# Projecting the first two units' attention values one unit at a time in 64 x 128 tiles of TensorE instead of two units at once in 64 x 32 tiles

## The chip, the cores and the metric

The kernel runs on one core of a Trainium2 chip. The metric is the device time of one execution in microseconds (us); several executions are timed and their median is given, and one more is recorded by the hardware profiler. All data are 32-bit floats.

## What is computed

The reference is one transformer block on two batches of 1024 tokens of 256 features: self-attention, cross-attention to a context of 154 tokens, and a gated feed-forward layer, each behind a layer norm and with a residual sum. Only the self-attention matters here:

```python
def _attention(xq, xkv, wq, wk, wv, wo, bo):
    q = (xq @ wq).reshape(B, S, N_HEADS, D_HEAD)
    k = (xkv @ wk).reshape(B, T, N_HEADS, D_HEAD)
    v = (xkv @ wv).reshape(B, T, N_HEADS, D_HEAD)
    attn = jnp.einsum('bihd,bjhd->bhij', q, k) * scale
    attn = jax.nn.softmax(attn, axis=-1)
    out = jnp.einsum('bhij,bjhd->bihd', attn, v).reshape(B, S, D_ATTN)
    return out @ wo + bo

h = _layernorm(x, ln1_g, ln1_b)
x = _attention(h, h, sa_wq, sa_wk, sa_wv, sa_wo, sa_bo) + x
```

There are 16 heads of 64 features, so `wq`, `wk` and `wv` are 256 x 1024.

## The kernel before, in words

The self-attention works in units. A unit is one batch and one pair of heads, so there are 16 units, and each needs 128 columns of queries, keys and values. The layer-normed and transposed activations of a batch lie in `hT`; its 128 partitions hold two halves of the tokens (partitions 0 to 63 and 64 to 127), each with its 256 features in four chunks of 64 (`NH` = 4). A projection therefore contracts over 64 rows at a time and uses the two halves of the array's rows for the two token halves.

Each unit is done in 8 steps `p` (two halves of 4), so unit 0 is steps 0 to 7, unit 1 steps 8 to 15. In one pass of the loop over `p` (L1294):

- `self_first(p)` (L676) multiplies queries with keys into two score tiles (`scores`, L491, on TensorE, "PE" in the profile), and VectorE (DVE) takes row maxima of each (L684). There are two score tiles in all, so the scores of a step wait until ScalarE (ACT) has done the exponents of the step before.
- The stores that the last step left behind are then issued (`flush(stores)`, L1301): copies from PSUM on ACT.
- `then()` issues the exponents (L509, ACT), the join of the step before on GpSimd (POOL) and ACT (`join`, L627), and the exchange of maxima and sums between partitions by four small DMAs on SyncE's (SP's) queue (L519).
- DVE turns the weighted exponents of earlier steps (`turn_group`, L647).
- `load_ahead` and the table `ahead` put weight loads on SP's queue: the keys' and queries' weights of unit 1 in steps 0 and 1 (L1286 and L1287).
- Last comes one larger piece of TensorE work: either half a unit's weighted sum of the values (`self_values`, L652, from step 7 on), or a piece from the list `work` (`run_work`, L573). Small side pieces, such as the context's keys (`context_keys`, L756) and a transposition of rows (L194), go along with the latter.

The order is written out by hand (`tc.manual_schedule`); each engine works through its own instructions in that order.

`work` begins with the second half of unit 0's queries (L1291) and two pieces of values (L1292); step 0 adds the queries and keys of unit 1 (`self_beside`, L697). So steps 0 to 4 each take one piece: queries of unit 0, values, values, queries of unit 1, keys of unit 1. Steps 5 and 6 find the list empty; step 6 adds the keys of two more pairs of heads for the cross-attention, one into a bank of the pool `sum_tile`, the other into one of `mm_tile`.

A piece of values (`project_self_values`, L394) takes a quarter of the tokens for two units at once: for each of two tiles of 128 tokens per half, four chunks, two halves and four groups of 32 tokens it multiplies 64 x 32 of `hT` (the stationary side) with 64 x 256 of `wv`. That is 64 matmuls in tiles of 64 rows by 32 columns of the array. Each matmul appears as two records in the trace. The result fills two PSUM banks (`two_banks`, L359); the pool `mm_tile` has only two, which queries, keys and values share, so a piece can begin only after the copies of the piece before. The store is four ACT copies of 256 columns to `held_v`, two for each unit. `held_v` has three places for units' values in turn (`unit_values`, L421) and a fourth that holds the current unit's values with the partition halves swapped (`move_values`, L424, in the sixth step of each unit). The weights `wv` are loaded for two units together, the next ones in step 7.

The prologue (L1260 to L1283) makes the first queries and keys with `project_both` (L362) in tiles of 64 rows by 128 columns, with 128 moving columns; line L369 in the profile.

Of the kernel before, what the change touches and what calls it, by code (L numbers as in the profile page):

```python
# [13 lines left out]
P = 128  # L14
# [4 lines left out]
def tile_transformer_block(ctx: ExitStack, tc: tile.TileContext, a: dict, out: bass.AP):  # L19
    nc = tc.nc  # L20
# [12 lines left out]
    GT = 4  # L33
    NG = NT // GT
    NC = D // P
    HR = P // 2
    NH = D // HR
# [32 lines left out]
    def mm_tile(name):  # L70
        return ps_m.tile([P, HB], F32, tag="mm", name=name)
# [25 lines left out]
    row_of, r = {}, 0  # L97
# [39 lines left out]
    wsl, wo = {}, {}  # L137
# [30 lines left out]
    for n in names[2:]:  # L168
        own = rows[row_of[n] - n_cols:row_of[n] - n_cols + n_of[n], :]
        p = HR if n in twice else P  # L170
# [45 lines left out]
    hT, vs, qk, oT = {}, {}, {}, {}  # L216
# [103 lines left out]
    def add_biases(kind, b):  # L320

        bo = {"sa": "sa_bo", "ca": "ca_bo", "ff": "ff_b2"}[kind]

        def add(t):
            xs = xt[b, t // GT][:, t % GT, :]
            nc.gpsimd.tensor_tensor(xs, xs, bias[bo], ALU.add)

        later.extend(lambda t=t: add(t) for t in range(NT))
        if b == B - 1 and kind != "ff":
            later.append(lambda: load_bias({"sa": "ca_bo", "ca": "ff_b2"}[kind]))  # L330

    def norm_beside(kind, b):

        after = {"sa": None, "ca": "sa", "ff": "ca"}[kind]
        stats, deviation, normalize, turn = norm_pieces(kind, b)
        n = 1 if narrow(kind, b) else 2
        lag = {}  # L340
        for fns, first in ((turn, 3), (stats, 0), (deviation, 1), (normalize, 2)):
            for i, fn in enumerate(fns):
                t = i if fns is stats else 2 * i + 1
                lag.setdefault(first + t // n, []).append((fn, fns is turn))
        for k in range(NT // n + 3):
            tiles = tile_order(kind)[k * n:(k + 1) * n]
            needs = [(after, b, half, t) for half in range(NQ) for t in tiles if after]

            def step(fns=lag[k]):
                slow.extend(fn for fn, _ in fns if fn in stats)  # L350
                done = [fn() for fn, _ in fns if fn not in stats]
                return next((fn for fn in done if fn), None)

            side.append((any(turns for _, turns in lag[k]), needs, step))
        if not narrow(kind, b):
            side.append((False, (), lambda: add_biases(kind, b)))


    def two_banks(name):  # L359
        return [mm_tile(f"{name}_{r}") for r in range(2)]  # L360

    def project_both(pq, wt, h, m, t0=0, n=S // 2, at=0):  # L362


        for c in range(NH):
            for f in range(0, P, m):
                for r in range(2):
                    own = slice(r * HR, (r + 1) * HR)
                    nc.tensor.matmul(  # L369
                        pq[r][f:f + m, at:at + n], lhsT=wt[own, c, f:f + m],  # L370
                        rhs=h[own, c, t0:t0 + n], start=(c == 0), stop=(c == NH - 1),
                        tile_position=(r * HR, f),
                    )

    def take_both(dst, pq, mul=None, t0=0, n=S // 2, shared=False):

        for r in range(2):
            k0, own = r * S // 2 + t0, pq[r][:, :n]
            if mul is not None:
                if shared and r:  # L380
                    nc.vector.tensor_scalar(
                        dst[:, k0:k0 + n], own, mul, 1.0, op0=ALU.mult, op1=ALU.mult)
                else:
                    nc.scalar.activation(dst[:, k0:k0 + n], own, AF.Copy, scale=mul)  # L384
                continue

            dk = dst.rearrange("p (h n j) -> p n h j", h=2, j=KB)[:, k0 // QG:(k0 + n) // QG]
            own = own.rearrange("p (n h j) -> p n h j", h=2, j=KB)
            if shared and r:
                nc.vector.tensor_copy(dk, own)  # L390
            else:
                nc.scalar.copy(dk, own)

    def project_self_values(b, pr, i):  # L394

        own = [unit_values(b, pr + j) for j in range(2)]
        pv = two_banks(f"pv_sa{b}_{pr}_{i}")
        wt, h = wsl["sa", pr, "v"], hT["sa", b]
        for e in range(2):
            for c in range(NH):  # L400
                for r in range(2):
                    half = slice(r * HR, (r + 1) * HR)
                    for f in range(0, P, KB):
                        t0 = (2 * i + e) * P + f
                        nc.tensor.matmul(  # L405
                            pv[r][f:f + KB, e * VC:(e + 1) * VC], lhsT=h[half, c, t0:t0 + KB],
                            rhs=wt[half, c, :], start=(c == 0), stop=(c == NH - 1),
                            tile_position=(r * HR, f),
                        )

        def store():
            for j in range(2):
                for r in range(2):
                    t0 = r * GT + 2 * i
                    nc.scalar.copy(
                        own[j][:, t0:t0 + 2, :],
                        pv[r].rearrange("p (e j d) -> p j e d", e=2, j=2)[:, j])

        return store

    def unit_values(b, pr):  # L421
        return held_v[:, (b * NPAIR + pr + 2) % 3]

# [7 lines left out]
    def costing(n, fn):  # L431

        fn.banks = n
        return fn

    def self_unit(b, pr):

        qk["sa", b, pr] = (
            p2.tile([P, S], F32, tag="QT", name=f"q_sa{b}_{pr}"),
            p2.tile([P, S], F32, tag="KT", name=f"k_sa{b}_{pr}"),  # L440
            (unit_values(b, pr), held_v[:, 3]),
        )

    def self_queries(b, pr, m=KB, t0=0):
        pq = two_banks(f"pq_sa{b}_{pr}")
        project_both(pq, wsl["sa", pr, "q"], hT["sa", b], m, t0, S // 2 - t0)
        return lambda: take_both(qk["sa", b, pr][0], pq, scale, t0, S // 2 - t0)

    def self_pieces(b, pr):


        def q():
            self_unit(b, pr)
            return self_queries(b, pr)

        def k():
            pk = two_banks(f"pk_sa{b}_{pr}")
            project_both(pk, wsl["sa", pr, "k"], hT["sa", b], KB)
            return lambda: take_both(qk["sa", b, pr][1], pk)

        return [costing(2, q), costing(2, k)]

    def value_piece(b, pr, i):
        return costing(2, lambda: project_self_values(b, pr, i))
# [20 lines left out]
    def out_order(kind):  # L485

        return [t for t in tile_order("ff" if kind == "ca" else "ca") if t % 2 == 0]
# [70 lines left out]
    work, outs = [], []  # L558
# [37 lines left out]
    def out_pieces(kind, b, half, tiles):  # L596
        outs.extend(lambda t=t: out_piece(kind, b, half, t) for t in tiles)

    units = [(b, pr) for b in range(B) for pr in range(NPAIR)]
# [97 lines left out]
    def self_beside(ui):  # L697

        nxt = self_pieces(*units[ui + 1]) if ui + 1 < NU else cross_pieces(*units[0])
        if ui + 1 < NU:  # L700
            if ui % 2 == 0 and ui:
                work.append(value_piece(*units[ui], 1))
            work.extend(nxt)
            if ui % 2:
                work.append(value_piece(*units[ui + 1], 0))
        else:

            work.extend(nxt[:1])
            held.extend(nxt[1:])
        if ui >= HP:  # L710
            ob, og = divmod((ui - HP) // HP, NQ)
            t0 = (ui % HP) * 2
            out_pieces("sa", ob, og, out_order("sa")[t0:t0 + 2])
        if ui == 1:
            norm_beside("sa", 1)
        if ui in (4, 6):
            add_biases("sa", (ui - 4) // 2)
        if ui == NPAIR + 1:
            norm_beside("ca", 0)
# [106 lines left out]
    def cross_pieces(b, pr):  # L826

        return [costing(2, lambda: cross_queries(b, pr, KB)), costing(1, lambda: context_values(b, pr))]
# [405 lines left out]
    with tc.manual_schedule():  # L1234
# [11 lines left out]
        own = [ps_s.tile([P, 2, HB], F32, tag="s", name=f"first_{r}") for r in range(2)]  # L1246
# [42 lines left out]
        side.extend((True, (), lambda pr=pr: context_keys(pr, sum_tile)) for pr in range(2))  # L1289
        side.append((True, (), turn_rows))  # L1290
        work.append(costing(2, lambda: self_queries(*units[0], P, 2 * P)))  # L1291
        work.extend(value_piece(*units[0], i) for i in range(2))  # L1292

        for p in range(SA):  # L1294
            if p % (2 * SH) == 0:
# [19 lines left out]
            h, hg = divmod(p, SH)  # L1315
            ui, n = divmod(p, 2 * SH)
# [6 lines left out]
            if hg == LAG:  # L1323
                f = (ui - NPAIR // 2 - 1) * EC
# [4 lines left out]
                if n == SH + LAG and ui in (0, 1, NU - 1):  # L1329

                    pr = {0: 2, 1: 4, NU - 1: 6}[ui]
# [3 lines left out]
        for c in range(CA):  # L1335
# [13 lines left out]
            ui, n = divmod(c, len(CG))  # L1349
# [83 lines left out]
        for k in range(2 * FU):  # L1433
            c = CA + k
# [17 lines left out]
            while n_left > 0 and sums:  # L1452
                fn, n = sums.pop(0)
# [51 lines left out]
```

## Time and profile before

| | |
|---|---|
| median of 3 runs | 1078.62 us (1077.93 to 1078.73) |
| profiled execution | 1076.39 us |
| its span, first to last instruction | 1074.6 us |
| PE busy / weight loads (PEld) busy | 1059.0 us (99%) / 711.8 us (66%) |
| DVE, ACT, POOL busy | 882.7, 645.5, 774.7 us |
| mean granted TensorE clock | 0.998 |
| values of the self-attention (L405) | 2048 records, 60.7 us |
| scores of the self-attention (L498) | 4096 records, 261.4 us |

The profile comes from one execution. "Busy" is the time in which an engine had an instruction in work. A row of a timeline or group names the source line, engine, output<-inputs, the tile of the array (rows*columns), the shape of the moving data and the number of records; brackets give how long the engine had stood before it, and what ended that. PEclk is the share of the full clock that TensorE was granted. The chain of waits is followed back from the last instruction of the execution. A DMA's landing is counted from its issue.

### The profile page before, as it was taken

How to read it: one execution, taken by the hardware profiler on the slowest of the kernel's cores; microseconds unless marked ns; L12 is line 12 of the kernel's file. 1: busy time of each engine (PE TensorE's matmuls, PEld its weight loads, DVE VectorE, ACT ScalarE, POOL GpSimd, SP SyncE). 2: the span in 40 equal slices, each digit the busy share in tenths (PEclk: the TensorE clock that was granted, in tenths of full speed). 3: DMA queues.
4: the chain of work that ended last, by engine and by line, in shares of the span. 5: the costliest groups of instructions: out<-in, count | busy, mean ns of one | idle time of the engine just before them, and what ended most of it. 6: DMA issues, size and time to landing. Idle time of an engine off the chain costs nothing.

```text
span 1074.6 us, 48887 instructions
## 1 busy us (share of the span) xinstructions
PE 1059.0 (99%) x20324; PEld 711.8 (66%) x20324; DVE 882.7 (82%) x1321; ACT 645.5 (60%) x2098; POOL 774.7 (72%) x1652
## 2 busy tenths in 40 slices
PE   8999999999999999999999999999999999999998
PEld 6366756656556655665775655566766667788998
DVE  5789999998989989999999899968877887655554
ACT  5666677677667666676776676665556564342331
POOL 2677777777777777677777777776666876499884
PEclk9999999999999999999999999999999999999999
DMA  3132121121121111111102101125776545000000
GB/s 101 31 79 54 25 67 48 24 73 26 30 50 42 34 47 33 44 33 34 44 14 53 44 14 38 33 54 137 173 180 166 124 107 114 16 5 16 20 10 30
DMA packets 86046, 60.97 MB, mean 57 GB/s; under 512 B 32122, under 2 KB 74562, under 8 KB 85826
## 3 DMA queue, kind: packets, MB, share of 16 engines
q1 hardware_dynamic: 84450, 57.07, 21.9%
q8 instruction: 160, 2.62, 1.0%
q10 hardware_dynamic: 1376, 0.79, 0.2%
q14 instruction: 60, 0.49, 0.2%
HBM read 27.91 MB, written 2.10 MB: 28 GB/s over the span
## 4 chain that ended last, share of the span: by engine, by line
PE 86%; DVE 3%; DMA 3%; POOL 3%; SPq 2%; issue 1%; ACT 1%; POOLq 0%; DVEq 0%; ACTq 0%
PE s L498 18%; PE po L550 18%; PE py_ca L472 5%; PE py_sa L472 5%; PE pv_sa L405 5%; PE pq_sa L369 5%; PE pk_sa L369 5%; PE poc L921 4%; PE pb L1042 4%; PE pq_ca L369 4%; PE pq L1187 3%; DMA st<-st 3%; PE sc L841 2%; PE pa L1042 2%; PE pc L1042 2%; SPq L519 2%
## 5 line engine op out<-in xcount | busy, mean ns | idle before, releaser
L622 POOL TENSOR_SCALAR p<-p,rd,ee 128x512 f32<-128x512 f32 x512 | 390.4, 768 | 97.7 <-DVE rd L612 97.3
L509 ACT ACTIVATE p<-s,st 128x512 f32<-128x512 f32 x512 | 345.0, 686 | 181.2 <-DVE st L684 177.6
L684 DVE TENSOR_REDUCE st<-s 128x2 f32<-128x1024 f32 x256 | 308.7, 1206 | 60.9 <-issue 22.7
L647 DVE STREAM_TRANSPOSE pT<-p 128x1024 f32<-128x1024 f32 x256 | 302.4, 1218 | 0.9 <-POOL p L622 0.9
L498 PE MATMUL s<-k_sa,q_sa 64*32 64x512 f32 x4096 | 261.4, 594 | 5.1 <-ACT p L509 4.4
L550 PE MATMUL po<-pT,held_v 64*32 64x256 f32 x8192 | 242.3, 376 | 0.9 <-DVE pT L647 0.5
L550 PEld LDWEIGHTS po<-pT,held_v 64*32 64x32 f32 x8192 | 178.8, 106 | 71.3 <-issue 22.6
L498 PEld LDWEIGHTS s<-k_sa,q_sa 64*32 64x32 f32 x4096 | 93.0, 107 | 94.8 <-issue 39.6
L858 ACT ACTIVATE p<-sc,neg 128x154 f32<-128x154 f32 x256 | 96.1, 404 | 79.2 <-DVE rden L866 75.2
L869 POOL TENSOR_SCALAR p<-p,rden 128x154 f32<-128x154 f32 x256 | 96.9, 399 | 51.7 <-DVE rden L866 51.4
L509 ACT ACTIVATION_READ_ACCUMULATOR p<-s,st 128x1 f32 x512 | 104.0, 203 | 0.0
L527 POOL TENSOR_TENSOR dd<-st 128x8 f32<-128x8 f32 x128 | 25.5, 200 | 66.8 <-DMA st<-st 63.0
L405 PE MATMUL pv_sa<-sa_wv,hT_ln 64*32 64x256 f32 x2048 | 60.7, 376 | 0.0
L472 PE MATMUL py_ca<-ca_wo,o_ca 128*128 128x256 f32 x256 | 60.2, 383 | 0.0
L472 PE MATMUL py_sa<-sa_wo,o_sa 128*128 128x256 f32 x256 | 59.7, 386 | 0.1
L847 DVE TENSOR_REDUCE neg<-sc 128x6 f32<-128x924 f32 (+1 forms) x48 | 47.8, 996 | 14.5 <-PE sc L841 14.5
L369 PE MATMUL pq_ca<-hT_ln,ca_wq 64*64 64x512 f32 (+1 forms) x544 | 59.1, 590 | 0.5 <-DVE st_ln L242 0.5
L472 PEld LDWEIGHTS py_sa<-sa_wo,o_sa 128*128 128x128 f32 x256 | 47.4, 190 | 18.1 <-issue 4.4
L369 PE MATMUL pk_sa<-hT_ln,sa_wk 64*32 64x512 f32 x960 | 57.5, 590 | 0.9 <-ACT q_sa L384 0.9
L369 PE MATMUL pq_sa<-hT_ln,sa_wq 64*32 64x512 f32 (+1 forms) x976 | 58.0, 586 | 0.0
L405 PEld LDWEIGHTS pv_sa<-sa_wv,hT_ln 64*32 64x32 f32 x2048 | 44.5, 106 | 18.1 <-issue 5.2
L858 ACT ACTIVATION_READ_ACCUMULATOR p<-sc,neg 128x1 f32 x256 | 56.5, 221 | 0.0
(155 smaller groups left out, 1471.9 us busy)
## 6 DMA issues: line engine op xcount, KB each, us to landing
wf<-pT_ca SPq DMA_DIRECT2D x128, 128.0 KB, 2.4
st<-st SPq DMA_DIRECT2D x512, 1.0 KB, 1.8
held_v<-held_v SPq DMA_DIRECT2D x32, 256.0 KB, 3.7
sa_wq<-in_L_xattn_sa_wq_dram SPq DMA_DIRECT2D x32, 128.0 KB, 3.6
sa_wk<-in_L_xattn_sa_wk_dram SPq DMA_DIRECT2D x32, 128.0 KB, 3.0
sa_wv<-in_L_xattn_sa_wv_dram SPq DMA_DIRECT2D x16, 256.0 KB, 4.5
ca_wq<-in_L_xattn_ca_wq_dram SPq DMA_DIRECT2D x32, 128.0 KB, 3.5
wf<-in_L_xattn_ff_w_dram SPq DMA_DIRECT2D x12, 256.0 KB
```

The costliest lines, as they stand in the source:

```text
L369: nc.tensor.matmul(pq[r][f:f + m, at:at + n], lhsT=wt[own, c, f:f + m], rhs=h[own, c, t0:t0 + n], start=(c == 0), stop=(c == NH - 1), tile ...
L405: nc.tensor.matmul(pv[r][f:f + KB, e * VC:(e + 1) * VC], lhsT=h[half, c, t0:t0 + KB], rhs=wt[half, c, :], start=(c == 0), stop=(c == NH - ...
L472: nc.tensor.matmul(py[:, e * D:(e + 1) * D], lhsT=o[:, i, (t + e) * P:(t + e + 1) * P], rhs=wo[kind][:, g * HP + i, :], start=(i == 0), st ...
L498: nc.tensor.matmul(sc[a4 * KB:(a4 + 1) * KB, j, :], lhsT=q[r, c:c + KB], rhs=k[r, h * HB:(h + 1) * HB], start=True, stop=True, tile_positi ...
L509: nc.scalar.activation(pr[:, j, :], sc[:, j, :], AF.Exp, bias=st[:, 0, 0, i, j:j + 1], accum_out=st[:, 0, 1, i, j:j + 1],)
L550: nc.tensor.matmul(po[a2][d:d + KB, :QH // 2], lhsT=v[e][r, t, d:d + KB], rhs=pT[r, d // DH * NK + n, :], start=(t == 0 and e == 0), stop= ...
L622: nc.gpsimd.tensor_scalar(pr[:, j, :], pr[:, j, :], own["rd"][:, c:c + 1], own["ee"][:, 0, c:c + 1], op0=ALU.mult, op1=ALU.mult,)
L647: nc.vector.transpose(halves[h][:, :, c:c + KB], slots[p]["p"][i].rearrange("p j (n k) -> p (j n) k", k=KB))
L684: nc.vector.tensor_reduce(st[:, 0, 0, i, :], sc[i], AX.X, ALU.max, negate=True)
L858: nc.scalar.activation(pr_[:, j, i, :T], sc[:, j, i * T:(i + 1) * T], AF.Exp, bias=neg[:, j, i:i + 1], accum_out=den[:, j, i:i + 1],)
L869: nc.gpsimd.tensor_scalar(pr_[:, j, i, :T], pr_[:, j, i, :T], rden[:, j, i:i + 1], 1.0, op0=ALU.mult, op1=ALU.mult,)
L1042: nc.tensor.matmul(into[:, :BT], lhsT=lhs, rhs=wh[pair][i], start=first, stop=True, skip_group_check=True)
```

## The change

The new function `project_unit_values` projects the values of one unit alone: the stationary side is 64 x 128 of `hT`, the moving side 64 x 128 of `wv`, in tiles of 64 rows by 128 columns of the array, `n` tiles of 128 tokens per half in one call. Its store copies `n` x 128 columns for each half. Unit 0 is done in two such pieces (two tiles of tokens each) in the places of the two old pieces. Unit 1 follows as one piece of four tiles of tokens behind the queries and keys of unit 1 in the list `work`. All later units are projected as before.

```diff
+    def project_unit_values(b, pr, i0, n):
+
+        own = unit_values(b, pr)
+        pv = two_banks(f"pv_sa{b}_{pr}_{i0}")
+        h, c0 = hT["sa", b], pr % 2 * P
+        wt = wsl["sa", pr - pr % 2, "v"][:, :, c0:c0 + P]
+        for i in range(i0, i0 + n):
+            for c in range(NH):
+                for r in range(2):
+                    half = slice(r * HR, (r + 1) * HR)
+                    nc.tensor.matmul(
+                        pv[r][:, i * P:(i + 1) * P], lhsT=h[half, c, i * P:(i + 1) * P],
+                        rhs=wt[half, c, :], start=(c == 0), stop=(c == NH - 1),
+                        tile_position=(r * HR, 0),
+                    )
+
+        def store():
+            for r in range(2):
+                t0 = r * GT + i0
+                nc.scalar.copy(
+                    own[:, t0:t0 + n, :],
+                    pv[r][:, i0 * P:(i0 + n) * P].rearrange("p (t d) -> p t d", d=P))
+
+        return store
+
@@ -459,6 +484,9 @@
+    def unit_value_piece(b, pr, i0, n):
+        return costing(2, lambda: project_unit_values(b, pr, i0, n))
 
     def value_piece(b, pr, i):
         return costing(2, lambda: project_self_values(b, pr, i))
@@ -701,6 +729,8 @@
             work.extend(nxt)
+            if ui == 0:
+                work.append(unit_value_piece(*units[1], 0, GT))
             if ui % 2:
                 work.append(value_piece(*units[ui + 1], 0))
@@ -1289,7 +1319,7 @@
         work.append(costing(2, lambda: self_queries(*units[0], P, 2 * P)))
-        work.extend(value_piece(*units[0], i) for i in range(2))
+        work.extend(unit_value_piece(*units[0], i, 2) for i in (0, 2))
```

## The prediction

> **What bounds the kernel now.** First the page: span, engines, chain.
>
> ```profile
> span 1074.6 us, 48887 instructions
> ...
> PE 1059.0 (99%) x20324; PEld 711.8 (66%) x20324; DVE 882.7 (82%) x1321; ACT 645.5 (60%) x2098; POOL 774.7 (72%) x1652
> ...
> PE 86%; DVE 3%; DMA 3%; POOL 3%; SPq 2%; issue 1%; ACT 1%; POOLq 0%; DVEq 0%; ACTq 0%
> ```
>
> TensorE (PE) is busy 99% and holds 86% of the chain that ended last. The changed work lies in the first 60 us, so I next read the timeline of PE there. Columns: start, length (us), engine, line, out<-in, tile, shape, count. One `matmul` of the code is two records.
>
> ```profile
> 9.47 1.16 PE L369 MATMUL first<-hT_ln,sa_wq 64*128 64x128 f32 x16
> 10.47 1.06 PE L369 MATMUL first<-hT_ln,sa_wk 64*128 64x128 f32 x16
> ...
> 17.51 1.95 PE L498 MATMUL s<-k_sa,q_sa 64*32 64x512 f32 x32 [0.65 <-DVE k_sa L390]
> 19.39 2.00 PE L369 MATMUL pq_sa<-hT_ln,sa_wq 64*128 64x256 f32 x16
> ...
> 21.99 1.96 PE L498 MATMUL s<-k_sa,q_sa 64*32 64x512 f32 x32
> 23.74 3.66 PE L405 MATMUL pv_sa<-sa_wv,hT_ln 64*32 64x256 f32 x128
> 27.33 1.34 PE L760 MATMUL pk<-ctxT,ca_wk 96*128 96x320 f32 x4
> 28.61 1.95 PE L498 MATMUL s<-k_sa,q_sa 64*32 64x512 f32 x32
> 30.35 3.66 PE L405 MATMUL pv_sa<-sa_wv,hT_ln 64*32 64x256 f32 x128
> 33.94 1.34 PE L760 MATMUL pk<-ctxT,ca_wk 96*128 96x320 f32 x4
> 35.21 1.95 PE L498 MATMUL s<-k_sa,q_sa 64*32 64x512 f32 x32
> 36.95 3.64 PE L369 MATMUL pq_sa<-hT_ln,sa_wq 64*32 64x512 f32 x64
> 40.52 0.24 PE L194 MATMUL p_rows<-ident,rows 28*128 28x28 f32 x1
> 40.69 1.97 PE L498 MATMUL s<-k_sa,q_sa 64*32 64x512 f32 x32
> 42.45 3.85 PE L369 MATMUL pk_sa<-hT_ln,sa_wk 64*32 64x512 f32 x64
> 45.89 2.13 PE L498 MATMUL s<-k_sa,q_sa 64*32 64x512 f32 x32
> 50.48 3.60 PE L498 MATMUL s<-k_sa,q_sa 64*32 64x512 f32 x32 [2.46 <-ACT p L509]
> 54.00 2.42 PE L760 MATMUL pk<-ctxT,ca_wk 96*128 96x320 f32 x8
> 56.35 1.95 PE L498 MATMUL s<-k_sa,q_sa 64*32 64x512 f32 x32
> ```
>
> Each row of scores (L498) opens a step p: p=0 at 17.51, p=1 at 21.99, then 28.61, 35.21, 40.69, 45.89, 50.48 (p=6), 56.35. In steps 1 to 4 PE has no gap: work of PE sets their length. Step 5 has scores alone, and PE stands 2.46 us until the exponents (ACT L509) free the score banks. The scores of step 6 then take 3.60 us where the others take 1.95. The windows of the trace show why (PEclk is the third column from the end):
>
> ```profile
> 47.05:50.46 3.41, 0.97 (x23) 0.06 (x7) 2.74 (x4) 1.89 (x6) 2.02 (x3) 1.00 0.04 4
> 50.46:53.88 3.42, 3.40 (x32) 0.62 (x32) 3.24 (x4) 1.42 (x6) 2.49 (x7) 0.50 0.02 3
> ```
>
> PE worked 0.97 of 3.41 us, and for the next 3.41 us the granted clock was 0.50. So the gap costs 2.46 us and 1.65 us more (3.60 - 1.95). The chain of waits passes there:
>
> ```profile
> 48.98 1.22 ACT p L509 x3
> ...
> 50.48 3.70 PE s L498 x32
> ...
> 54.20 1.24 DVE st L684
> ...
> 55.47 0.03 ACT p L509
> ```
>
> Later, from 102.3 us on, PE has hardly a gap, so I take time won before it as kept to the end:
>
> ```profile
> 102.30:700.00 597.70, 595.76 (x14592) 364.61 (x14596) 551.35 (x630) 411.49 (x1236) 448.75 (x933) 1.00 0.16 39
> ```
>
> **The change, part by part.**
>
> *Removed:* the two 64*32 pieces of steps 1 and 2, from start to next start 3.59 us each (27.33 - 23.74 and 33.94 - 30.35), 7.18 us.
>
> *Added:* unit 0 alone in steps 1 and 2 (16 matmuls, 32 records each), unit 1 in step 5 (64 records), as 64*128 tiles with 128 moving columns. The trace has this very form: 16 records take 1.00 us from 9.47 to 10.47, so 62.5 ns each. That is 2.0, 2.0 and 4.0 us, together 8.0: PE does 0.8 us more, but 4.0 of it where it stood.
>
> *Change of tile shape:* scores overlap the 64*32 values by 0.21 us (21.99 + 1.96 - 23.74), and a 64*128 piece by 0.07 (17.51 + 1.95 - 19.39). I charge 0.13 us at the start of each new piece; between 0 and 0.2.
>
> The Trainium skill, "TensorE: Matmul & The Clock Gate", section "LDWEIGHTS (loading the stationary operand)", speaks against this form: a weight load costs its columns over 1.2 GHz, so 107 ns for 128 columns. By it alone the pieces would take 3.4, 3.4 and 6.8 us, and the time would be near 1080.7; the trace's 62.5 ns, load included, disagrees. What the loads could do here is weighed below from rows.
>
> *Steps 1 to 3.* I add up starts with today's lengths: scores 1.75, keys of the context (L760) 1.28. Step 1: values 23.87 to 25.87, keys to 27.15. Step 2: scores 27.15, values 29.02 to 31.02, keys to 32.29. Step 3: scores 32.29, done 34.03; today 36.95. That is 2.92 us earlier. The other engines allow it: today ScalarE (ACT) and VectorE (DVE) wait here for PE:
>
> ```profile
> 28.08 1.17 ACT L415 COPY held_v<-pv_sa 128x256 f32<-128x256 f32 x4
> ...
> 31.06 0.69 ACT L509 ACTIVATE p<-s,st 128x512 f32<-128x512 f32 x1 [1.48 <-DVE st L684]
> ```
>
> ```profile
> 29.80 1.22 DVE L684 TENSOR_REDUCE st<-s 128x2 f32<-128x1024 f32 x1 [4.26 <-PE s L498]
> ```
>
> Two copies instead of four also take 0.58 us off ACT in steps 2 and 3. It stood there, so that earns nothing.
>
> *Then a new wait.* Unit 1's queries (36.95 today) need their weights, issued by SyncE (SP) behind the exchange of step 1, which waits for exponents that don't move. Nothing on SP's or POOL's queue is added, removed or reordered.
>
> ```profile
> 31.04 1.34 SPq L134 DMA_DIRECT2D sa_wq<-in_L_xattn_sa_wq_dram  x2
> ```
>
> ```profile
> DMA to landing us min/median/max: 4.0/4.0/4.0
> ```
>
> The second of the two is issued at about 31.7 and lands at 35.7. Today that is early; now PE arrives at 34.03 and waits 1.7 us. All of PE's queue stands behind it. Could it land sooner? Fetches of instructions share the DMA engines, and one falls into this transfer:
>
> ```profile
> q8 instruction: 160, 2.62, 1.0%
> ```
>
> ```profile
> q8 instruction: 1, 0.02, 59.9%
> ```
>
> ```profile
> q8 instruction: 1, 0.02, 65.4%
> ```
>
> The page's 160 packets over 40,648 records of PE and its loads are one per 254. The last two rows are the windows 24.05-24.15 and 33.30-33.40: one packet in each. Counted on from 24.1 in the new order (values 64 records with loads, keys 8, scores 64, values 64, keys 8, together 208), the 254th falls into step 3's scores, near 33.5. So the fetch again meets the transfer, and I keep 35.7. The other end is no wait at all.
>
> *Steps 3 to 5:* queries 35.75, rows 39.32, scores 39.49, keys 41.25, scores 44.69: 1.2 us earlier than today's 45.89. Unit 1's values run from 46.57 to 50.57. They use the two banks of the keys, whose copies (two of 512 columns) end 1.2 us after the keys do:
>
> ```profile
> 46.38 1.07 ACT L392 COPY k_sa<-pk_sa 128x512 f32<-128x512 f32 x2 [0.29 <-PE pk_sa L369]
> ```
>
> That is 45.9, before 46.57. Unit 1's own copies, two of this size, lie at 50.8 to 51.9, and step 6's exponents, queued behind them on ACT, aren't due before 53; without that cover they would cost 1.07 us.
>
> *Step 6:* scores start at 50.65 (today 50.48), but PE has had no 2.46 us gap, so I take the full clock: done at 52.6, today 54.08, 1.5 us earlier. DVE's two reductions start at 51.8 and 53.1 (1.22 us and the reciprocal between them later), today 54.20 for the second: 1.1 us. The second pair of exponents follows at 54.4 instead of 55.47, also 1.1. The chain continues from these exponents through the exchanges on SP, so the gain is 1.1 to 1.5 us: I take **1.2 us**.
>
> For the profiled execution (span 1074.6, 1076.39 us in all) that gives 1075.2; the median of the shown runs is 2.23 us higher, and from it the forecast is **1077.4 us**.
>
> **The rivals.**
>
> *The weights aren't waited for.* The fetch may miss the transfer. Queries then start at 34.03 to 34.5, everything after 1.2 to 1.7 us earlier still; exponents of step 5 (due 1.4 us after the reduction that follows step 5's scores) would still be ready first. Gain 2.3 to 2.8 us, about 1076.0. For: the transfer itself, without the fetch, could be done soon after the second issue. Against: the landing row and the count above.
>
> *Nothing is won.* In an execution whose clock isn't halved in step 6 today, its scores end at 52.43; the new ones end at 52.6. Then the 1.1 to 1.5 us are gone, and the time is about 1078.7. The Trainium skill, same page, section "Part 1: The HAM clock gate (the "warmup" mystery)", says the activity window is free-running and a kernel's throttled stretch run-variable. The trace's 3.41 us stretch fits the window, but one profile can't show how often it comes. For this rival: 2.46 us of a 3.41 us window may be split by the next window's edge.
>
> *The clock is halved at the new wait* (slower). PE stands about 1.5 us at 34.2. If that suffices, the next 3.41 us run at half clock, 1.7 us lost. Step 6's scores then end at 54.3 instead of 54.08, DVE's second reduction starts 0.65 us later than today: 1079.3, and about 1080.5 where today's clock isn't halved. It decides when such a gap fills enough of a window: today 2.44 us did, and the 0.65 us ahead of 17.51 did not (scores in 1.95).
>
> *The 64*128 form is bound by its weight loads* (slower).
>
> ```profile
> L472 PEld LDWEIGHTS py_sa<-sa_wo,o_sa 128*128 128x128 f32 x256 | 47.4, 190 | 18.1 <-issue 4.4
> ```
>
> A load of 128 columns lasts 190 ns in this row. With the two half-height tiles side by side that is 95 ns a record. Units take 3.0, 3.0 and 6.1 us; queries start at 36.1, unit 1 runs from 46.9 to 53.0, step 6's scores end at 55.0, DVE's second reduction starts 1.4 us later than today: 1080.0, and 1081.4 where today's clock isn't halved. Break-even is where unit 1 ends at about 52.1: (52.1 - 46.57) / 64 = 86 ns. Against: both 16-record rows at 1.00 us.
>
> That the change wouldn't do what it says is excluded by the new order of PE's instructions: 32 + 32 matmuls of 128 columns in steps 1, 2 and 5, before and after the same neighbours.
>
> **How the numbers follow.** Chances: forecast 0.47, weights in time 0.25, nothing won 0.12, clock at the new wait 0.09, bound by loads 0.07. The range 1075.6 to 1079.8 holds the first three with the bounds of the unknown costs (the switches, the landing), and part of the fourth. About what a measurement of this kernel can tell from no change is 0.2%, 2.16 us. Faster by more, below 1076.46: most of the second case and the upper tail of the first, 0.32. Slower by more, above 1080.78: most of the last two, since both grow by the 1.2 to 2 us that a run without a halved clock today would lack, 0.12. Within: 0.56.
>
> **What would show it.** In the profile after: values in steps 1 and 2 in 2.0 us each, 4.0 in step 5 (bound by loads: over 5.5); a gap of PE near 34 to 36 that a DMA of sa_wq ends (none: second case); step 6's scores in 1.95 us, starting within 0.3 us of 50.6; PEclk 1.00 around 50 us, and at 36 to 40. The prediction is wrong if step 7's scores don't start 1.1 to 1.5 us before 56.35, or if these are given back before 102.3 us, where PE's unbroken work begins.

## The result, and the profile after

| | before | after |
|---|---|---|
| median | 1078.37 us (16 runs, 1076.98 to 1083.05) | 1074.86 us (16 runs, 1070.62 to 1076.90) |
| ratio | | 0.9963, 95% interval 0.9952 to 0.9974 |
| profiled execution / its span | 1076.39 / 1074.6 us | 1075.05 / 1073.2 us |

The ratio is a gain of 4.0 us (2.8 to 5.2), and the medians lie 3.5 us apart; 1.2 was forecast, and 1074.86 lies 0.7 us under the range. The direction was right and the size was not. The two profiled executions are 1.3 us apart, because that of before was faster than all 16 timed runs of its kernel.

The page of the kernel after, span, engines and chain:

```profile
span 1073.2 us, 48628 instructions
...
PE 1059.4 (99%) x20196; PEld 716.2 (67%) x20196; DVE 883.1 (82%) x1321; ACT 646.9 (60%) x2096; POOL 777.0 (72%) x1652
...
PE 74%; DMA 7%; SPq 6%; POOL 6%; DVE 2%; issue 2%; ACT 1%; POOLq 0%; DVEq 0%; ACTq 0%
```

PE's busy time is the same (1059.0 before): no work of PE was saved. The chain's shares are shown for completeness, and nothing below rests on them. The timeline of PE after (start, length, as before) shows where the time came from:

```profile
17.71 1.95 PE L526 MATMUL s<-k_sa,q_sa 64*32 64x512 f32 x32 [0.64 <-DVE k_sa L390]
...
24.09 2.06 PE L431 MATMUL pv_sa<-sa_wv,hT_ln 64*128 64x128 f32 x32
...
29.22 2.12 PE L431 MATMUL pv_sa<-sa_wv,hT_ln 64*128 64x128 f32 x32
...
32.54 1.95 PE L526 MATMUL s<-k_sa,q_sa 64*32 64x512 f32 x32
34.28 3.64 PE L369 MATMUL pq_sa<-hT_ln,sa_wq 64*32 64x512 f32 x64
...
43.22 2.13 PE L526 MATMUL s<-k_sa,q_sa 64*32 64x512 f32 x32
45.29 4.04 PE L431 MATMUL pv_sa<-sa_wv,hT_ln 64*128 64x128 f32 x64
49.26 1.95 PE L526 MATMUL s<-k_sa,q_sa 64*32 64x512 f32 x32
...
53.48 2.21 PE L526 MATMUL s<-k_sa,q_sa 64*32 64x512 f32 x32
```

This execution starts 0.20 us later (17.71 against 17.51). Against the rows of before, that start taken off, step 3's scores come 2.87 us earlier (32.54, before 35.21), step 5's also 2.87 (43.22, 45.89), step 6's 1.42 (49.26, 50.48) and step 7's 3.07 (53.48, 56.35). Steps 1 and 2 win 2.9 us; unit 1's piece spends 4.0 us in step 5, where PE had stood 2.46 us and then run at half clock.

A little is added later, ahead of unit 2's keys. The same row before and after (each ends where its window ended or another row began, so only starts and waits are to be compared):

```profile
75.01 1.57 PE L369 MATMUL pk_sa<-hT_ln,sa_wk 64*32 64x512 f32 x17 [0.95 <-ACT q_sa L384]
```

```profile
71.67 3.72 PE L369 MATMUL pk_sa<-hT_ln,sa_wk 64*32 64x512 f32 x57 [0.23 <-ACT q_sa L384]
```

75.01 - 71.67 + 0.20 = 3.54 us. In this one profile of after some 1.5 us of that are lost again between 610 and 770 us, by the starts of VectorE's instructions, which come in the same order in both. A second profile of the same kernel, below, is 3.6 us shorter at its end, so the change itself need not give them back.

### The profile page after: what moved, and what is told of

It is laid out like the page before. It is cut to its first block, busy times and chain, and to the rows that moved or that the text cites. A ratio compares the mean times of both kernels' runs of the same rounds, so it can differ in the third digit from the quotient of the medians.

```text
span 1073.2 us, 48628 instructions
## 1 busy us (share of the span) xinstructions
PE 1059.4 (99%) x20196; PEld 716.2 (67%) x20196; DVE 883.1 (82%) x1321; ACT 646.9 (60%) x2096; POOL 777.0 (72%) x1652
## 4 chain that ended last, share of the span: by engine, by line
PE 74%; DMA 7%; SPq 6%; POOL 6%; DVE 2%; issue 2%; ACT 1%; POOLq 0%; DVEq 0%; ACTq 0%
PE s L526 14%; PE po L578 13%; DMA st<-st 7%; SPq L547 6%; PE py_ca L500 5%; PE py_sa L500 4%; PE poc L951 4%; PE pq_ca L369 4%; PE pq_sa L369 4%; PE pb L1072 4%; PE pk_sa L369 4%; PE pq L1217 3%; PE pv_sa L405 3%; POOL p L650 3%; PE sc L871 2%; PE pa L1072 2%
## 5 line engine op out<-in xcount | busy, mean ns | idle before, releaser
L526 PE MATMUL s<-k_sa,q_sa 64*32 64x512 f32 x4096 | 257.8, 591 | 2.8 <-ACT p L537 2.0
L578 PEld LDWEIGHTS po<-pT,held_v 64*32 64x32 f32 x8192 | 182.5, 106 | 67.0 <-issue 26.0
L526 PEld LDWEIGHTS s<-k_sa,q_sa 64*32 64x32 f32 x4096 | 89.7, 106 | 93.1 <-issue 46.6
L915 DVE STREAM_TRANSPOSE pT_ca<-p 128x480 f32<-128x480 f32 (+1 forms) x96 | 52.9, 587 | 0.9 <-POOL p L899 0.8
L405 PE MATMUL pv_sa<-sa_wv,hT_ln 64*32 64x256 f32 x1792 | 52.9, 376 | 0.0
```

The lines of the kernel that those rows point to most:

```text
L405: nc.tensor.matmul(pv[r][f:f + KB, e * VC:(e + 1) * VC], lhsT=h[half, c, t0:t0 + KB], rhs=wt[half, c, :], start=(c == 0), stop=(c == NH - ...
L526: nc.tensor.matmul(sc[a4 * KB:(a4 + 1) * KB, j, :], lhsT=q[r, c:c + KB], rhs=k[r, h * HB:(h + 1) * HB], start=True, stop=True, tile_positi ...
L578: nc.tensor.matmul(po[a2][d:d + KB, :QH // 2], lhsT=v[e][r, t, d:d + KB], rhs=pT[r, d // DH * NK + n, :], start=(t == 0 and e == 0), stop= ...
```

## The experiments

The theory after the result: steps 1 and 2 are paced by PE's work; the change moves some of it into the one step where PE stood, and nothing new is waited for. The rivals: the gain comes from the halved clock of step 6, or from the tile's form, or the weights of unit 1's queries are waited for after all. Each run was timed against the kernel before on the same chip. Where a kernel's functions have moved, its line numbers differ from those of before.

### e1_fill: the clock alone

```diff
@@ before, in the loop over p, after run_work(...)
+            if p == 5:
+                warm = mm_tile("warm")
+                for _ in range(14):
+                    nc.tensor.transpose(warm[:, :P], ident, ident)
```

> The kernel before with 14 transpositions of the identity into an unused PSUM bank at the end of step 5, in the gap of 2.46 us in which PE stood; their result is not used. If the gain came chiefly from the halved clock of step 6 (1.65 us in the profile of before), the time is 1.2 to 1.7 us under before. If moving the work is what counts, nothing but a part of that 1.65 us is won, and over many executions less (the clock is not halved in each): 0 to 1.0 us under before. PEclk at 50 to 54 us should be 1.00, and step 6's scores 1.95 us, by both.

Measured: 1078.87 us, ratio 1.0004 (0.9992 to 1.0017). PE's timeline:

```profile
48.18 1.75 PE L1326 MATMUL warm<-ident 128*128 128x128 f32 x14
50.72 1.09 PE L498 MATMUL s<-k_sa,q_sa 64*32 64x512 f32 x16 [0.80 <-ACT p L509]
52.06 1.09 PE L498 MATMUL s<-k_sa,q_sa 64*32 64x512 f32 x16 [0.24 <-ACT p L509]
...
55.43 2.30 PE L498 MATMUL s<-k_sa,q_sa 64*32 64x512 f32 x32
57.52 1.07 PE L550 MATMUL po<-pT,held_v 64*32 64x256 f32 x24
59.08 3.01 PE L550 MATMUL po<-pT,held_v 64*32 64x256 f32 x100 [0.49 <-DMA held_v<-held_v]
```

The gap shrinks to 0.80 us and step 6's scores run at full clock: 1.09 us for each half, with 0.24 between. Step 7's scores start at 55.43 instead of 56.35. But the weighted values (L550) then wait for the move of unit 0's values, a DMA issued behind step 5's exchange, which the clock does not hasten, and step 8's scores start as before. Ahead of unit 2's keys this profile is 1.0 us ahead once more, since the wait of 0.95 us there is gone; by 170 us 0.3 us of that is left, and the times show no gain.

The runs of before say about the same. Of 69 executions in three calls, 15 show a mean granted clock of 1.000; their median is 1077.5 us in each call. The 53 with a mean below 0.999 have medians of 1078.1, 1078.5 and 1078.5. Taken together, a halved clock goes with 0.8 us (95% interval 0.0 to 1.2, by resampling), not with the 1.65 that one row suggests. The mean does not say where the clock was halved, but one stretch of 3.41 us at half in 1075 us makes 0.998, and the kernels that run unit 1's values in step 5 without a forced wait (the changed one, e2_tile32, e4_swap, e8_swap, e9_split, e10_tile64) show a mean below 0.999 in only 4 of 61 executions.

### e3_form: the form alone

```diff
@@ before, project_self_values
-                    for f in range(0, P, KB):
+                    m = P if (b, pr) == units[0] else KB
+                    for f in range(0, P, m):
@@ and KB in the slices of pv and h there becomes m
```

> The old order with the first two pieces (both units at once) in tiles of 64 x 128 and 256 moving columns: 32 records a piece instead of 128. By the row of unit 0's second half of queries (16 records of this form in 1.93 us) a piece takes 3.86 us instead of 3.59, so if only the place counts the time is 0 to 0.6 us above before, and step 5's gap and step 6's halved clock stay. If the tile's form were what the change gains by, the time would be near the changed kernel's, some 3 us under before.

Measured: 1077.56 us, ratio 0.9997 (0.9988 to 1.0006).

```profile
24.16 3.72 PE L406 MATMUL pv_sa<-sa_wv,hT_ln 64*128 64x256 f32 x32
...
51.17 1.09 PE L499 MATMUL s<-k_sa,q_sa 64*32 64x512 f32 x16 [2.46 <-ACT p L510]
```

A piece of values holds half of a batch's tokens (two tiles of 128 of the four in each half; a quarter was said above). It takes 3.72 us in 32 records, where 128 records of 64*32 took 3.66. The gap of step 5 is as before. The form alone gains nothing that can be told.

### e2_tile32: the new places with the old tile

```diff
@@ after, project_unit_values
+                    for f in range(0, P, KB):
+                        nc.tensor.matmul(pv[r][f:f + KB, i * P:(i + 1) * P],
+                            lhsT=h[half, c, i * P + f:i * P + f + KB], ..., tile_position=(r * HR, f))
```

> The changed order (unit 0 in steps 1 and 2, unit 1 in step 5) with the old tiles of 64 x 32 and 128 moving columns: 128 records for a piece of unit 0, 256 for unit 1. If the place alone counts and records cost by columns (28 ns x 1/2), the pieces take 1.8, 1.8 and 3.6 us and the time is that of the changed kernel or up to 0.5 us less. If the cost is per record (28 ns each, bound by weight loads or issue), they take 3.6, 3.6 and 7.2 us: steps 1 and 2 stay as before and step 5 grows by 3.2 us more than in the changed kernel, so the time is about 1080, slower than before by 1 to 2 us.

Measured: 1078.06 us, ratio 0.9996 (0.9983 to 1.0008). Neither price was right:

```profile
24.00 1.95 PE L432 MATMUL pv_sa<-sa_wv,hT_ln 64*32 64x128 f32 x120
26.72 0.42 PE L432 MATMUL pv_sa<-sa_wv,hT_ln 64*32 64x128 f32 x8 [0.77 <-issue]
...
30.09 1.47 PE L432 MATMUL pv_sa<-sa_wv,hT_ln 64*32 64x128 f32 x82
32.32 0.91 PE L432 MATMUL pv_sa<-sa_wv,hT_ln 64*32 64x128 f32 x46 [0.76 <-issue]
...
46.83 3.68 PE L432 MATMUL pv_sa<-sa_wv,hT_ln 64*32 64x128 f32 x232
51.76 0.53 PE L432 MATMUL pv_sa<-sa_wv,hT_ln 64*32 64x128 f32 x20 [1.24 <-issue]
```

Records go out every 16 ns (1.95 us / 120), and then PE stops three times with nothing to wait for ("issue"): 0.77, 0.76 and 1.24 us. The pieces take 3.1, 3.1 and 5.2 us, and the whole gain is gone. The place alone does not pay: it depends on the form.

### e10_tile64: half as many records

The same edit with `HR` (64) in place of `KB` (32).

> The changed order in tiles of 64 x 64 with 128 moving columns: 64 records for a piece of unit 0 and 128 for unit 1, half of what the 64 x 32 tiles needed and twice the changed kernel's. If the gaps of the 64 x 32 run (0.77, 0.76 and 1.24 us that no wait explains, after some 500 records and loads had been issued faster than elsewhere) come from instructions that arrive too slowly, they shrink to under 0.3 us here, the pieces take 1.9 to 2.2 us and 4 us, and the time is that of the changed kernel within 0.7 us. If small tiles cost by record, 28 ns each, it is the same; if by column tile, the pieces take 2.5 us and more and the time is 1 to 2 us above the changed kernel.

Measured: 1074.76 us, ratio 0.9973 (0.9962 to 0.9984).

```profile
23.92 1.98 PE L432 MATMUL pv_sa<-sa_wv,hT_ln 64*64 64x128 f32 x64
...
45.00 3.72 PE L432 MATMUL pv_sa<-sa_wv,hT_ln 64*64 64x128 f32 x128
48.65 1.95 PE L528 MATMUL s<-k_sa,q_sa 64*32 64x512 f32 x32
```

No such stop in these pieces, which take 2.0 and 3.7 us, and most of the gain is back. That the stops of e2_tile32 come from instructions arriving too slowly fits both runs, and the trace of e2_tile32 supports it: packets of the queue "q8 instruction" end at 25.32, 30.90 and 50.49 us, and PE goes on 1.40, 1.42 and 1.27 us after these. No run changed the supply of instructions alone.

### e4_swap and e8_swap: are the queries' weights waited for?

```diff
@@ after
-        ahead[0] = lambda: load_weights("sa", units[1][1], "k")
-        ahead[1] = lambda: load_weights("sa", units[1][1], "q")
+        ahead[0] = lambda: load_weights("sa", units[1][1], "q")
+        ahead[1] = lambda: load_weights("sa", units[1][1], "k")
```

> The changed kernel with the loads of unit 1's queries' and keys' weights exchanged on SP's queue (queries first), so that the queries' weights land near 29 us and cannot be waited for; the keys' weights land near 34 to 36 and are used at 39.8. By the step of the prediction that failed (queries wait until 35.7), this would be 1.2 to 1.7 us faster than the changed kernel. If the weights are not waited for in the changed kernel, it is the same within 0.4 us: about 1074.9, 0.996 to 0.998 of before.

Measured: 1072.90 us (5 runs), ratio 0.9959 (0.9947 to 0.9972). That left the question open, so the kernel ran again beside the changed kernel:

> The changed kernel with the two loads exchanged once more (queries' weights first). Its first five runs had a median of 1072.9 where sixteen of the changed kernel had 1074.9, from different calls. If queries' weights are waited for in some executions of the changed kernel, this stays 1 to 2 us below the run of the changed kernel beside it. If they never are, the two agree within 0.5 us.

> The changed kernel once more, on the same chip and beside the next one, to compare the two directly: 1073.5 to 1075.5, 0.995 to 0.9975 of before.

Measured: e8_swap 1073.43 us, ratio 0.9960 (0.9946 to 0.9974); e7_after 1073.99 us, ratio 0.9963 (0.9949 to 0.9978). Side by side the two cannot be told apart: their medians are 0.56 us apart, less than the intervals. With five and six runs that would not exclude a wait of 1.2 us in some executions; it is the rows that speak against it. The queries' row of after, above, has none, and the rows of e7_after show none, neither at the queries nor, above 0.2 us, at unit 2's keys:

```profile
33.94 3.64 PE L369 MATMUL pq_sa<-hT_ln,sa_wq 64*32 64x512 f32 x64
```

```profile
71.24 3.72 PE L369 MATMUL pk_sa<-hT_ln,sa_wk 64*32 64x512 f32 x57 [0.17 <-ACT q_sa L384]
```

Its span is 1071.0 us, 3.6 under the profile of before.

### e5_late: the weights made late

```diff
@@ after
-        ahead[1] = lambda: load_weights("sa", units[1][1], "q")
+        ahead[2] = lambda: load_weights("sa", units[1][1], "q")
```

> The changed kernel with the load of the weights of unit 1's queries issued one step later on SP's queue (in step 2, behind that step's exchange, so near 35 us; by the 2.7 us to landing of the changed kernel's profile they land near 39). The queries are ready to start at 34.3 and then wait 4 to 5 us. If time won or lost ahead of step 3 passes one for one to the end (what I now hold), the time is 4 to 5 us above the changed kernel, 0.5 to 1.5 us above before. If what counts is only that step 5's gap is filled, the loss is smaller, under 2 us, and the time stays below 1077.

Measured: 1080.44 us, ratio 1.0023 (1.0007 to 1.0038), 6.5 us above e7_after on the same chip. PE's timeline, and a window with the granted clock:

```profile
38.20 5.89 PE L369 MATMUL pq_sa<-hT_ln,sa_wq 64*32 64x512 f32 x64 [3.51 <-DMA sa_wq<-in_L_xattn_sa_wq_dram]
...
59.22 2.21 PE L526 MATMUL s<-k_sa,q_sa 64*32 64x512 f32 x32
```

```profile
38.50:41.90 3.40, 3.40 (x33) 1.50 (x39) 0.14 (x1) 0.65 (x3) 1.15 (x3) 0.50 0.03 5
```

The wait is 3.51 us, and the queries behind it run at half clock: 5.89 us instead of 3.64. Together 5.8, and step 7's scores start 5.74 us later than in the changed kernel (59.22, 53.48; 5.57 if each start is taken off). The medians, 6.5 us apart, show no less: time lost ahead of step 3 is not made up later when step 5 is filled.

### e6_step6: unit 1 one step later

```diff
@@ after: unit 1's piece is not added in self_beside, but in the loop over p
+            if p == 6:
+                work.append(unit_value_piece(*units[1], 0, GT))
```

> The changed kernel with unit 1's piece in step 6 instead of step 5, so that PE stands in step 5 as before (about 2.5 us) while the exponents of step 5, the exchange behind them and the move of unit 0's values keep the 2.7 us that steps 1 and 2 win. If the gain is carried by those (the chain through SP and the move), the time is that of the changed kernel, near 1075. If PE must have its gap filled, step 7's scores start 2 to 3.5 us later than in the changed kernel and most is lost: 1077 to 1078.5.

Measured: 1077.86 us, ratio 0.9996 (0.9984 to 1.0009).

```profile
43.24 2.13 PE L526 MATMUL s<-k_sa,q_sa 64*32 64x512 f32 x32
47.82 1.09 PE L526 MATMUL s<-k_sa,q_sa 64*32 64x512 f32 x16 [2.45 <-ACT p L537]
...
50.18 3.84 PE L431 MATMUL pv_sa<-sa_wv,hT_ln 64*128 64x128 f32 x64
...
56.30 1.95 PE L526 MATMUL s<-k_sa,q_sa 64*32 64x512 f32 x32
```

Steps 1 to 4 win the same (step 5 at 43.24), PE stands in step 5, and step 7 starts at 56.30, as before (56.35): step 6 spends what they won. The earlier exponents and exchanges alone carry nothing that can be told: the gap has to be filled. The profiled execution is the fastest of the 12 (1075.05 us), so its later rows say little of the median.

### e9_split: half in step 5, half in step 6

```diff
@@ after, self_beside
-                work.append(unit_value_piece(*units[1], 0, GT))
+                work.extend(unit_value_piece(*units[1], i, 2) for i in (0, 2))
```

> The changed kernel with unit 1's piece cut in two halves of 2.0 us, one in step 5 and one in step 6. Step 6's scores can then start near 47.8 (when step 5's exponents free the banks) instead of 49.3, so step 6's maxima, exponents and exchange are up to 1.4 us earlier; PE loses 0.5 us of gap, and step 7's scores start 0.5 to 0.8 us later than in the changed kernel. If the exchanges through SP set the time from here to unit 2, the gain is up to 1 us over the changed kernel (1073 to 1074); if PE's own work sets it, the loss is 0.5 to 0.8 us (1075 to 1075.5).

Measured: 1075.02 us, ratio 0.9974 (0.9964 to 0.9983).

```profile
54.05 1.34 PE L790 MATMUL pk<-ctxT,ca_wk 96*128 96x320 f32 x4 [0.59 <-ACT held_v L440]
55.33 1.95 PE L526 MATMUL s<-k_sa,q_sa 64*32 64x512 f32 x32
```

Step 6's scores start at 47.77, but the context's keys now wait for the bank of the second half, and step 7 starts 1.85 us later than in the changed kernel. Its ratio lies above that of e7_after, with overlapping intervals. In this profile PE's own gaps set the time, not the exchanges; no version beat the changed kernel clearly.

## Why the prediction was wrong, point by point

- **Steps 1 to 3: right.** 62.5 ns a record, pieces of 2.0 us and a charge of 0.13 us for the tile's change gave 2.92 us at step 3; measured 2.87. The rule of the Trainium skill that a weight load costs its columns over 1.2 GHz ("TensorE: Matmul & The Clock Gate", "LDWEIGHTS (loading the stationary operand)") is not what this form costs per record: 64 records took 4.04 us, 63 ns each. But a single load is no cheaper than the rule has it. In the profile of after the 128 loads of these pieces (PEld, L431) last 188 ns on average, about three times the distance of the records, so several must be in work at once; "load included" in the prediction was right of the records and not of a load.
- **The new wait: wrong, and this is the step that failed.** "So the fetch again meets the transfer, and I keep 35.7." I counted one instruction fetch per 254 records and loads on from 24.1 and put it at 33.5. In the profile after, it comes at 35.2 (one packet in the window 35.15 to 35.25), and the queries' weights, issued at 30.7 and 31.4, land 2.7 us after the second issue, at 34.1. The rows are the share of the instruction queue in that window, and the time to landing of these loads, both of the kernel after:

```profile
q8 instruction: 1, 0.02, 88.9%
```

```profile
DMA to landing us min/median/max: 2.7/2.7/2.7
```

  The queries start at 34.28, right behind the scores. Two terms of the wait were off. The landing took 2.7 us instead of 4.0, because the load's last packet had ended at 33.74, before the fetch began. And the issue came 0.5 us earlier (31.40 against 31.74, each start taken off): the exponents of step 1 did not move, but the exchange between them and the load took 2.47 us instead of 3.34. A page's mean distance of fetches was used as a clock for one fetch; in the trace of before the distances between neighbouring fetches run from 160 to 351 records and loads. In e7_after the fetch did come at 33.35, near the place foreseen, and even so met nothing: the load's last packet had ended at 33.04. The wait was mis-sized by its whole 1.7 us; 1.2 + 1.7 = 2.9 us would have been the forecast without it.
- **The rival "the weights aren't waited for": this is what happened,** though priced at 2.3 to 2.8 us. Its sum ended at step 7. The wait ahead of unit 2's keys (0.95 before, 0.17 to 0.23 after) adds 0.7, which makes 3.0 to 3.5. The profiles of after and e7_after give 3.5 and 3.7 at those keys (each counted from its own start), the latter's end 3.6; the measured 4.0 (2.8 to 5.2) holds that, though single profiles of one kernel differ by 2 us at their ends.
- **Steps 5 and 6: right but for the time.** The values run from 45.29 to 49.3 with no gap ahead, 1.5 us sooner than foreseen if the later start is taken off, and step 6's scores run at full clock. Step 7's scores come 3.07 us earlier, not 1.1 to 1.5, which the prediction had itself named as the sign of being wrong. e6_step6 shows that filling this step is what lets the time of steps 1 and 2 pass.
- **The rival "nothing is won": refuted.** It priced the halved clock at the full 1.1 to 1.5 us gain. e1_fill, at full clock in 8 of its 12 executions, wins nothing that can be told, and executions of before at full clock are only some 0.8 us faster.
- **The two slower rivals: not seen in the changed kernel.** The form was not bound by its loads. The halved clock at the new wait did come where e5_late forced the wait, with a price of 2.2 us on the queries.
- **The chances** gave 0.32 to faster by over 0.2%, and 0.47 to a case that hung on one landing. With a landing that depends on where one fetch falls, the case without a wait deserved at least as much.

## What to carry to other kernels

An engine that is busy 99% can still have one step in which it stands, and moving existing work there is worth the time that it frees in the steps that it leaves, as long as nothing else holds these steps. Price such a move by the gap that it fills and by what PE waits for next, step by step, up to the point where PE's work is unbroken. Work that is cut smaller to be moved needs a form with few instructions: the same values in the same places were worth 4.0 us in 128 records, 2.9 in 256 (not told apart from 4.0) and nothing in 512.

## What the runs showed of the hardware

- **Small tiles can stop PE without a wait.** At 16 ns a record (64*32, 128 moving columns) PE stopped for 0.77, 0.76 and 1.24 us with no wait in the trace, and went on 1.3 to 1.4 us after an instruction packet ended; at 31 ns (64*64: 1.98 us / 64) it did not stop. Instructions that arrive too slowly are the likely cause.
- **A weight load lands late when an instruction packet falls into it.** The same load of the queries' weights, 512 packets, landed 2.7 to 3.0 us after its last issue in the profiles of after, e6_step6, e7_after, e9_split and e10_tile64, 3.5 in e3_form, and 3.9 to 4.2 in those of before, e1_fill and e2_tile32. In the last four its final packets (16, in e3_form 14) come one at a time, and the first of these starts within 0.02 us of the end of an instruction packet: 34.38 and 34.40 in before, 34.93 and 34.94 in e1_fill, 34.60 and 34.62 in e2_tile32, 33.68 and 33.68 in e3_form. In the other five no instruction packet starts while the load's packets run. (Instruction packets are those of the queues "q8 instruction" and "q14 instruction"; the ones that fell into a load lasted 0.3 to 1.3 us.) No run moved a fetch alone.
- **A gap of 2.46 us halves the clock in some executions and not in others.** In the profile of before it did; in e3_form's and e6_step6's, with gaps of 2.46 and 2.45 us, it did not. Over all executions, the mean clock lay below 1.000 in 54 of 69 of before, 10 of 11 of e3_form and 9 of 12 of e6_step6. The window of e3_form behind its gap (PEclk third from the end):

```profile
51.17:54.60 3.43, 3.18 (x36) 1.20 (x37) 3.43 (x5) 1.73 (x6) 2.70 (x8) 1.00 0.02 3
```

  The Trainium skill says that the activity window is free-running ("TensorE: Matmul & The Clock Gate", "Part 1: The HAM clock gate (the "warmup" mystery)"). These counts agree with that: the same gap then falls differently into the window from one execution to the next.
